# Gathers, node work and the last sums of a graph layer: where the copy of x runs and how the last two chunks are cut

## The chip, the cores and the metric

The kernel runs on one core of a Trainium2 chip. The metric is the device time of one execution in microseconds (us). Before the change the median of three runs is 1359.61 us (1357.78 to 1359.88). A core has five engines with queues of their own: TensorE (PE: matrix products and transposes), VectorE (DVE), ScalarE (ACT), GpSimd (POOL) and SyncE (SP, which here only issues DMAs).

## The reference

A layer on a graph of N = 8192 nodes with C = 256 channels and E = 131072 edges sorted by target, in float32 throughout:

```python
ea = edge_attr @ w_e + b_e
msg = jax.nn.relu(x[src] + ea)
agg = jax.ops.segment_sum(msg, dst, num_segments=N)
t = x + agg
h_local = _bn(jax.nn.relu(t @ w1 + b1) @ w2 + b2 + x, bn1_g, bn1_b)
# attention inside groups of 32 nodes, 4 heads
h_attn = _bn(attention(x) @ out_w.T + out_b + x, bn2_g, bn2_b)
out = h_local + h_attn
out = _bn(out + (jax.nn.relu(out @ m_w1 + m_b1) @ m_w2 + m_b2), bn3_g, bn3_b)
return _layernorm(x + out)
```

So each edge fetches the row of its source node, adds its own 64 features times `w_e` and a bias, takes a relu, and is summed into its target. Attention needs x alone; the dense layers need the sums.

## The kernel before, in words

**Edges** go in NB = 128 blocks of 1024. Since targets are sorted, block b touches about 64 nodes, and its sums fall into a window of 160 nodes that begins 48 before node 64 b. For each block, `gather` (L112) has POOL issue 8 indirect DMAs (L117) of 128 rows of 1 KB each into a buffer `xs` (5 buffers). `load_edges` (L127) loads the features of two blocks at once (`ea`, 2 buffers). `edge_transpose` (L410) turns them on PE and ACT copies them out. `edge_products` (L419) multiplies by `w_e` on PE (L428), DVE adds the gathered rows (L430) and ACT takes the relu (L433), each in two halves. `edge_sums` (L436) sums on PE with one-hot matrices that DVE makes (L440, L449), and ACT copies the result (`ws`, L454). `edge_place` (L457) moves the sums into the node window by another one-hot product (L463, L468), and DVE adds them to the transposed x of the chunk (L478), for two blocks together except for the last two blocks.

**The bias b_e** is added in one of two ways. `copy_x` (L482) makes a copy `xb` of x with b_e added: a chunk of 512 nodes is loaded (L491), DVE adds `be` (L492), and it is stored to HBM (L486). Gathers of blocks from NX = 13 on read `xb`. The first 13 blocks read x itself, and DVE adds `be` to each half of their messages (L432, two instructions a block). `copy_x(i)` handles two chunks, so all 16 chunks are called for within blocks 0 to 8. Its tiles share the buffers of tiles of the dense layers (tags h1, zT, and y with two buffers).

**Nodes** go in 16 chunks of 512. `attention` (L237) and `dense` (L335) are generators: they yield after each piece with a price in us. `Work` (L494) keeps two streams of them, attention in one and dense in the other, and `run(us)` hands out pieces by turns until the amount is used up. A piece that yields `LATER` (after the softmax on DVE) lets its stream rest for three calls of `run`. `dense` can do a part of a chunk: tiles `t_a` to `t_z` of its four tiles of 128 nodes. Its layers are at L344, ACT's relus at L351 and L360, DVE's adds at L354 and L369, its transposes at L381, the layer norm at L384 to L392, its store at L395.

**Order.** On PE the instructions run in the order in which the program is written (`manual_schedule`, L537). On the other engines and in the DMA queues a scheduler orders them at build time, and each then runs strictly in that order. The main loop (L546) handles block b so: load the features of b + 2, copy x, gather b + 2, products of b, a third of `PER` (4.875 us) of node work, sums of b - 1, a third, transpose of b + 2, a third, and place all sums up to b - 2 (up to b - 1 from block 126 on). The dense layers of chunk c - 1 enter at block 8 c + 4, so those of chunk 14 at block 124; chunk 15 enters in parts at the ends of blocks 126, 127 and 128.

At the start `srcd` (L58) holds the source indices of the first two blocks, which the first 16 gathers read. Those of all other blocks come out of the setup as `srci`.

Of the kernel before, what the change touches and what calls it, by code (L numbers as in the profile page):

```python
# [9 lines left out]
FP = mybir.dt.float32  # L10
# [8 lines left out]
P = 128  # L19
N, C, E, ED, H, NPG = 8192, 256, 131072, 64, 4, 32  # L20
DH = C // H
KC = C // P
BE = 1024
NB = E // BE
NH = 4
WN = P // NH
TJ = BE // NH // P
TB = NH * TJ
NPB = N // NB
WB = 160  # L30
WL = 48
CH = 512
NCH = N // CH
BPC = NB // NCH
TN = CH // P
GT = P // NPG
NX = 13
ND = 2
AGG_ROWS = N + 2 * P
TE = 8  # L40
# [9 lines left out]
def gnn_kernel(ctx: ExitStack, tc: tile.TileContext, x, src, dst, edge_attr, w, out):  # L50
    nc = tc.nc
# [3 lines left out]


    srcd = const.tile([P, ND * NH, TJ], I32, name="srcd")
    nc.sync.dma_start(srcd, src[0 : ND * BE].rearrange("(g p j) -> p g j", p=P, j=TJ))  # L58


    ident = const.tile([P, P], FP, name="ident")
# [8 lines left out]
    xb = dram.tile([N, C], FP, name="xb")  # L70
# [8 lines left out]
    w1 = const.tile([P, KC, C], FP, name="w1")  # L79
    w2 = const.tile([P, KC, C], FP, name="w2")  # L80
    mw1 = const.tile([P, KC, 2 * C], FP, name="mw1")
    mw2 = const.tile([P, 2 * KC, C], FP, name="mw2")
# [24 lines left out]
    npool = fast.enter_context(tc.tile_pool(name="node", bufs=1))  # L107
# [4 lines left out]
    def gather(b):  # L112
        xs = epool.tile([P, NH, TJ, C], FP, name="xs", tag="xs", bufs=5)
        for h in range(NH):
            for j in range(TJ):
# [3 lines left out]
                    out_offset=None,  # L119
                    in_=x if b < NX else xb[:, :],  # L120
                    in_offset=bass.IndirectOffsetOnAxis(ap=idx, axis=0),
# [213 lines left out]
    def dense(n0, st, pool, bank, t_a=0, t_z=TN):  # L335

        nt = t_z - t_a
        cs, ts, part = slice(t_a * P, t_z * P), slice(t_a, t_z), nt / TN
        xn, tT, hA = st["xn"][:, ts, :], st["xT"][:, :, cs], st["hA"][:, :, cs]

        def layer(wt, nk, o, act):
            ps = bank()[:, : nt * P]
            for k in range(nk):
                nc.tensor.matmul(  # L344
                    ps, wt[:, k, o * P : (o + 1) * P], act[:, k, :], start=(k == 0), stop=(k == nk - 1)
                )
            return ps

        h1 = pool.tile([P, KC, CH], FP, name="h1", tag="h1")[:, :, : nt * P]
        for o in range(KC):  # L350
            nc.scalar.activation(h1[:, o, :], layer(w1, KC, o, tT), AF.Relu, bias=v_("b1", o))  # L351
            yield 1.7 * part
        for o in range(KC):
            nc.vector.scalar_tensor_tensor(  # L354
                hA[:, o, :], layer(w2, KC, o, h1), s1[:, o : o + 1], hA[:, o, :], op0=ALU.mult, op1=ALU.add
            )
            yield 1.7 * part
        m1 = pool.tile([P, 2 * KC, CH], FP, name="m1", tag="m1")[:, :, : nt * P]
        for o in range(2 * KC):
            nc.scalar.activation(m1[:, o, :], layer(mw1, KC, o, hA), AF.Relu, bias=v_("m_b1", o))  # L360
            yield 1.7 * part
        zT = pool.tile([P, KC, CH], FP, name="zT", tag="zT")[:, :, : nt * P]
        for o in range(KC):

            nc.scalar.activation(
                zT[:, o, :], hA[:, o, :], AF.Identity, scale=s3[:, o : o + 1], bias=c3[:, o : o + 1]
            )
        for o in range(KC):
            nc.vector.scalar_tensor_tensor(  # L369
                zT[:, o, :], layer(mw2, 2 * KC, o, m1), s3[:, o : o + 1], zT[:, o, :], op0=ALU.mult, op1=ALU.add  # L370
            )
            yield 3.4 * part
        y = pool.tile([P, TN, C], FP, name="y", tag="y", bufs=2)[:, :nt, :]
        st6 = pool.tile([P, TN, 6], FP, name="st", tag="st")
        mv = pool.tile([P, TN, 2], FP, name="mv", tag="mv")
        for t2 in range(0, nt, 2):
            n2 = min(2, nt - t2)
            ps = bank()[:, : n2 * C].rearrange("p (t c) -> p t c", t=n2)
            for t in range(n2):
                for k in range(KC):  # L380
                    nc.tensor.transpose(  # L381
                        ps[:, t, k * P : (k + 1) * P], zT[:, k, (t2 + t) * P : (t2 + t + 1) * P], ident
                    )
            nc.vector.tensor_add(y[:, t2 : t2 + n2, :], ps, xn[:, t2 : t2 + n2, :])  # L384
        for t in range(nt):
            nc.vector.bn_stats(st6[:, t, :], y[:, t, :])
            nc.vector.bn_aggr(mv[:, t, :], st6[:, t, :])
        rstd = pool.tile([P, TN], FP, name="rstd", tag="rstd")
        nc.scalar.activation(rstd[:, :nt], mv[:, :nt, 1], AF.Sqrt, bias=eps_t)
        nc.vector.reciprocal(rstd[:, :nt], rstd[:, :nt])  # L390
        for t in range(nt):
            nc.vector.tensor_scalar(  # L392
                y[:, t, :], y[:, t, :], mv[:, t, 0:1], rstd[:, t : t + 1], ALU.subtract, ALU.mult
            )
        nc.sync.dma_start(out[ds(n0 + t_a * P, nt * P), :].rearrange("(t p) c -> p t c", p=P), y)  # L395
        yield 0.9 * part
# [3 lines left out]
    chunk = [{} for _ in range(NCH)]  # L400

    def bank():
        return pps.tile([P, CH], FP, name="at", tag="at", bufs=2)
# [75 lines left out]

    xp_of = {}  # L480

    def copy_x(i):  # L482

        for c in range(2 * i - 2, 2 * i):
            if c >= 0:
                nc.sync.dma_start(xb[c * CH : (c + 1) * CH, :].rearrange("(p t) c -> p t c", p=P), xp_of.pop(c))  # L486
        for c in range(2 * i, min(2 * i + 2, NCH)):

            tag = ("h1", "y", "zT", "y")[c % 4]
            xp = xp_of[c] = npool.tile([P, TN, C], FP, name="xp", tag=tag, bufs=2 if tag == "y" else 1)  # L490
            nc.sync.dma_start(xp, x[c * CH : (c + 1) * CH, :].rearrange("(p t) c -> p t c", p=P))  # L491
            nc.vector.tensor_add(xp, xp, be[:, None, :].to_broadcast([P, TN, C]))  # L492

    class Work:  # L494
# [20 lines left out]
        def run(self, us):  # L515
            self.owed += us
            for i in range(2):
                self.rest[i] = max(self.rest[i] - 1, 0)
            while self.owed > 0:
                ready = [i for i in (self.turn, 1 - self.turn) if self.streams[i] and not self.rest[i]]  # L520
                if not ready:
                    break
                t = self.piece(ready[0])
                if t == LATER:
                    self.rest[ready[0]] = 3
                elif t is not None:
                    self.owed -= t
                    self.turn = 1 - ready[0]
            self.owed = min(self.owed, 2.0)
# [5 lines left out]
    work = Work()  # L535
    PER = 39.0 / BPC
    with tc.manual_schedule(engines={PE}):  # L537
        first = [attention(c * CH, chunk[c], npool, bank, bank2) for c in range(2)]
        for g in first:
            next(g)  # L540
        for g in first:
            work.add(0, g)
        edge_transpose(0)
        edge_transpose(1)
        placed = 0
        for b in range(NB + 1):  # L546
            if b + 2 < NB:
                load_edges(b + 2)
            if b <= NCH // 2:
                copy_x(b)  # L550
            if 4 <= b < 8:
                wt, name = ((w1, "w1"), (w2, "w2"), (mw1, "m_w1"), (mw2, "m_w2"))[b - 4]
                nc.sync.dma_start(wt, w[name].rearrange("(k p) m -> p k m", p=P))
            if b + 2 < NB:
                gather(b + 2)
            c, at = divmod(b, BPC)
            if at == 0 and 1 <= c < NCH - 1:
                work.add(0, attention((c + 1) * CH, chunk[c + 1], npool, bank, bank2))
            if at == 4 and 1 <= c < NCH:
                work.add(1, dense((c - 1) * CH, chunk[c - 1], npool, bank))  # L560
            if b < NB:
                edge_products(b)
            work.run(PER / 3)
            if b >= 1:
                edge_sums(b - 1)
            if b < NB:
                work.run(PER / 3)
            if b + 2 < NB:
                edge_transpose(b + 2)
            if b < NB:  # L570
                work.run(PER / 3)

            while placed <= (b - 2 if b < NB - 2 else b - 1):
                edge_place(placed)
                placed += 1
            if b == NB - 2:
                work.add(1, dense((NCH - 1) * CH, chunk[NCH - 1], npool, bank, 0, 2))
            if b == NB - 1:
                work.add(1, dense((NCH - 1) * CH, chunk[NCH - 1], npool, bank, 2, 3))
        work.add(1, dense((NCH - 1) * CH, chunk[NCH - 1], npool, bank, 3, 4))  # L580
        work.finish()
    fast.close()

# [120 lines left out]
```

## Time and profile before

The profile is of one execution that took 1364.3 us, of which the recorded span is 1362.5 us; the median of the plain runs is 1359.61 us.

| engine | busy us | share of the span | instructions |
|---|---|---|---|
| PE | 1242.5 | 91% | 7939 |
| POOL | 995.5 | 73% | 1032 |
| DVE | 743.0 | 55% | 1218 |
| ACT | 662.5 | 49% | 1014 |

The page cuts the span into 40 slices of 34 us. In the first three the DMA engines are busy for 8 or 9 tenths and more (283, 361 and 352 GB/s moved), afterwards for 4 or 5 tenths. PE is busy 9 tenths or more from the ninth slice on to the fourth from the end. POOL is at 7 tenths in nearly all slices and falls to 4 and 0 in the last two. The mean clock granted to PE is 0.977.

How to read it: "L117" is line 117 of the kernel. Groups of instructions give the count, the busy time, the mean of one in ns, and the idle time ahead of them with what ended it. "Issue" as a reason means that the engine waited for nothing that the profile shows. In the timelines each row gives start, duration, engine, line, operation, and in brackets the idle time before it.

### The profile page before, as it was taken

How to read it: one execution, taken by the hardware profiler on the slowest of the kernel's cores; microseconds unless marked ns; L12 is line 12 of the kernel's file. 1: busy time of each engine (PE TensorE's matmuls, PEld its weight loads, DVE VectorE, ACT ScalarE, POOL GpSimd, SP SyncE). 2: the span in 40 equal slices, each digit the busy share in tenths (PEclk: the TensorE clock that was granted, in tenths of full speed). 3: DMA queues.
4: the chain of work that ended last, by engine and by line, in shares of the span. 5: the costliest groups of instructions: out<-in, count | busy, mean ns of one | idle time of the engine just before them, and what ended most of it. 6: DMA issues, size and time to landing. Idle time of an engine off the chain costs nothing.

```text
span 1362.5 us, 20476 instructions
## 1 busy us (share of the span) xinstructions
PE 1242.5 (91%) x7939; PEld 738.2 (54%) x7939; DVE 743.0 (55%) x1218; ACT 662.5 (49%) x1014; POOL 995.5 (73%) x1032
## 2 busy tenths in 40 slices
PE   2778979899999999999999999999999999999797
PEld 2445545555556555555555555555556565565455
DVE  5687665545556463645546464555645555545452
ACT  1444444545555564545546465454645455554332
POOL 6877777777777777777777777777777777777740
PEclk9889989899999999999999999999999999999899
DMA  8994445445454454545454454544545454454421
GB/s 283 361 352 116 130 117 160 141 136 153 135 169 137 126 161 136 167 136 152 136 148 138 137 165 137 151 136 140 162 123 167 135 164 123 137 148 123 137 62 33
DMA packets 141443, 206.73 MB, mean 152 GB/s; under 512 B 19710, under 2 KB 103964, under 8 KB 141340
## 3 DMA queue, kind: packets, MB, share of 16 engines
q0 software_dynamic: 49152, 134.28, 34.6%
q1 hardware_dynamic: 90768, 69.75, 16.0%
q10 hardware_dynamic: 1420, 1.33, 0.3%
q8 instruction: 64, 1.05, 0.3%
q14 instruction: 39, 0.32, 0.1%
HBM read 188.51 MB, written 16.78 MB: 151 GB/s over the span
## 4 chain that ended last, share of the span: by engine, by line
PE 43%; POOL 23%; issue 12%; DVE 8%; DMA 8%; ACT 5%; SPq 0%; DVEq 0%; POOLq 0%; ACTq 0%
POOL xs L117 23%; PE at L344 15%; PE pe L428 8%; DMA xs<-xb,srci 6%; PE pw L449 4%; PE at L256 4%; DVE msg L430 3%; PE l L468 3%; PE at L266 2%; PE at L327 2%; PE tp L414 2%; ACT msg L433 2%; PE at L315 1%; DVE bd L307 1%; ACT pr L292 1%
## 5 line engine op out<-in xcount | busy, mean ns | idle before, releaser
L117 POOL DMA_INDIRECT xs<-xb,srci x920 | 879.3, 956 | 280.3 <-issue 264.5
L433 ACT ACTIVATE msg<-msg 128x1024 f32<-128x1024 f32 x256 | 269.4, 1056 | 361.1 <-DVE msg L430 309.7
L430 DVE TENSOR_TENSOR msg<-pe,xs 128x1024 f32<-128x1024 f32 x256 | 303.5, 1219 | 62.6 <-PE pe L428 44.0
L428 PE MATMUL pe<-we,eaT 64*128 64x256 f32 x2048 | 263.8, 397 | 1.1 <-ACT pr L292 0.8
L428 PEld LDWEIGHTS pe<-we,eaT 64*128 64x128 f32 x2048 | 190.6, 191 | 46.7 <-issue 20.2
L449 PE MATMUL pw<-msg,oh 128*32 128x256 f32 x2048 | 139.1, 390 | 0.0
L344 PE MATMUL at<-hA,mw 128*128 128x512 f32 (+2 forms) x288 | 127.8, 567 | 5.8 <-DVE hA L354 5.4
L256 PE MATMUL at<-xT,inT 128*128 128x512 f32 x256 | 126.0, 615 | 5.9 <-DVE y L384 4.0
L344 PE MATMUL at<-m,mw 128*128 128x512 f32 (+2 forms) x288 | 117.9, 554 | 6.6 <-ACT xT L246 6.5
L117 POOL DMA_INDIRECT xs<-in_x_dram,srci x88 | 98.7, 1121 | 26.8 <-issue 26.2
L416 ACT COPY eaT<-tp 128x512 f32<-128x512 f32 x128 | 74.5, 582 | 86.7 <-PE tp L414 86.1
L414 PE MATMUL tp<-ident,ea 128*128 128x128 f32 x512 | 81.4, 282 | 35.4 <-ACT ws L454 32.4
L414 PEld LDWEIGHTS tp<-ident,ea 128*128 128x128 f32 x512 | 60.6, 143 | 92.4 <-ACT ws L454 56.6
L449 PEld LDWEIGHTS pw<-msg,oh 128*32 128x32 f32 x2048 | 54.0, 110 | 100.6 <-issue 45.0
L468 PEld LDWEIGHTS l<-oh,ws 128*128 128x128 f32 x512 | 82.3, 195 | 39.5 <-issue 36.9
L440 DVE TENSOR_TENSOR oh<-iota_n,rel 128x256 f32<-128x256 f32 x128 | 54.1, 423 | 75.7 <-PE pw L449 75.6
L468 PE MATMUL l<-oh,ws 128*128 128x160 f32 x512 | 94.2, 308 | 0.5 <-ACT ws L454 0.5
L369 DVE SCALAR_TENSOR_TENSOR zT<-at,s,zT 128x512 f32<-128x512 f32 (+2 forms) x36 | 24.9, 692 | 123.4 <-PE at L344 122.1
L463 DVE TENSOR_SCALAR oh<-iota_n,wrow 128x160 f32<-128x160 f32 x128 | 41.6, 325 | 84.9 <-PE l L468 84.8
L344 PEld LDWEIGHTS at<-m,mw 128*128 128x128 f32 x288 | 49.9, 190 | 57.9 <-issue 45.8
L478 DVE TENSOR_TENSOR xT<-l,xT 128x352 f32<-128x352 f32 (+3 forms) x95 | 42.2, 464 | 62.6 <-PE l L468 62.4
L344 PEld LDWEIGHTS at<-hA,mw 128*128 128x128 f32 x288 | 47.5, 190 | 50.4 <-issue 34.1
(106 smaller groups left out, 1313.8 us busy)
## 6 DMA issues: line engine op xcount, KB each, us to landing
ea<-in_edge_attr_dram SPq DMA_DIRECT2D x64, 512.0 KB, 4.5
xs<-xb,srci POOLq DMA_INDIRECT x920
xn<-in_x_dram SPq DMA_DIRECT2D x16, 512.0 KB, 5.0
xp<-in_x_dram SPq DMA_DIRECT2D x16, 512.0 KB, 6.5
xb<-xp SPq DMA_DIRECT2D x16, 512.0 KB
out_dram<-y SPq DMA_DIRECT2D x15, 512.0 KB, 3.2
xs<-in_x_dram,srci POOLq DMA_INDIRECT x88
mw<-in_L_gnn_m_w_dram SPq DMA_DIRECT2D x2, 512.0 KB
```

Of the source, the lines that this page charges most:

```text
L117: nc.gpsimd.indirect_dma_start(out=xs[:, h, j, :], out_offset=None, in_=x if b < NX else xb[:, :], in_offset=bass.IndirectOffsetOnAxis(ap= ...
L256: nc.tensor.matmul(ps, inT[:, k, o * P : (o + 1) * P], xT[:, k, :], start=(k == 0), stop=(k == KC - 1))
L344: nc.tensor.matmul(ps, wt[:, k, o * P : (o + 1) * P], act[:, k, :], start=(k == 0), stop=(k == nk - 1))
L414: nc.tensor.transpose(tp[:, h, :], ea[:, h, :], ident)
L416: nc.scalar.copy(eaT, tp)
L428: nc.tensor.matmul(pe[:, i, u, :], eaT[rows, h + u, :], we[rows, :], start=True, stop=True)
L430: nc.vector.tensor_add(half, pe, xs[:, h : h + 2].rearrange("p u i c -> p i u c"))
L433: nc.scalar.activation(msg[:, h : h + 2], msg[:, h : h + 2], AF.Relu)
L440: nc.vector.tensor_tensor(oh, iota_n[:, None, :WN].to_broadcast([P, TB, WN]), rel[:, b, :, None].to_broadcast([P, TB, WN]), ALU.is_equal,)
L449: nc.tensor.matmul(pw[h * WN : (h + 1) * WN, :], oh[:, h * TJ + j, :], msg[:, h, j, :], start=(j == 0), stop=(j == TJ - 1),)
L468: nc.tensor.matmul(l2[:, k, odd * NPB : odd * NPB + WB], ws[:, k * P : (k + 1) * P], oh2, start=(not odd and k == 0), stop=bool(odd or alo ...
L478: nc.vector.tensor_add(xT, l2[:, :, a - n : z - n], xT)
```

## The change

Six edits go together.

1. `NX` is 22 instead of 13: nine more blocks gather from x and have their bias added on DVE (L432).
2. `srcd` is loaded by two DMAs, the half of block 0 from SP and that of block 1 from ACT.
3. `copy_x` handles one chunk a block over blocks 0 to 16, with the tags h1 and zT alone, one buffer each. The loads of the four dense weights move from blocks 4 to 7 to blocks 7 to 10.
4. Within a block the transposes of b + 2 stand behind both pieces of node work (a third and two thirds of the amount, in two calls), and a resting stream rests for two calls. In the last 8 blocks the amount is 1.3 times as large.
5. The sums of b - 1, not b - 2, are placed from block 116 on.
6. Chunk 14's dense layers run in two halves that enter as soon as their sums are placed (ends of blocks 118 and 122), chunk 15's as before in parts.

```diff
-NX = 13
+NX = 22
...
-    nc.sync.dma_start(srcd, src[0 : ND * BE].rearrange("(g p j) -> p g j", p=P, j=TJ))
+    for b in range(ND):
+        (nc.sync, nc.scalar)[b].dma_start(
+            srcd[:, b * NH : (b + 1) * NH, :], src[b * BE : (b + 1) * BE].rearrange("(g p j) -> p g j", p=P, j=TJ)
+        )
...
-    def copy_x(i):
-
-        for c in range(2 * i - 2, 2 * i):
-            if c >= 0:
-                nc.sync.dma_start(xb[c * CH : (c + 1) * CH, :].rearrange("(p t) c -> p t c", p=P), xp_of.pop(c))
-        for c in range(2 * i, min(2 * i + 2, NCH)):
-
-            tag = ("h1", "y", "zT", "y")[c % 4]
-            xp = xp_of[c] = npool.tile([P, TN, C], FP, name="xp", tag=tag, bufs=2 if tag == "y" else 1)
+    def copy_x(c):
+
+        if c >= 1:
+            nc.sync.dma_start(xb[(c - 1) * CH : c * CH, :].rearrange("(p t) c -> p t c", p=P), xp_of.pop(c - 1))
+        if c < NCH:
+
+            xp = xp_of[c] = npool.tile([P, TN, C], FP, name="xp", tag=("h1", "zT")[c % 2])
             nc.sync.dma_start(xp, x[c * CH : (c + 1) * CH, :].rearrange("(p t) c -> p t c", p=P))
             nc.vector.tensor_add(xp, xp, be[:, None, :].to_broadcast([P, TN, C]))
...
                 if t == LATER:
-                    self.rest[ready[0]] = 3
+                    self.rest[ready[0]] = 2
...
-            if b <= NCH // 2:
+            if b <= NCH:
                 copy_x(b)
-            if 4 <= b < 8:
-                wt, name = ((w1, "w1"), (w2, "w2"), (mw1, "m_w1"), (mw2, "m_w2"))[b - 4]
+            if 7 <= b < 11:
+                wt, name = ((w1, "w1"), (w2, "w2"), (mw1, "m_w1"), (mw2, "m_w2"))[b - 7]
...
+            per = PER if b < NB - 8 else 1.3 * PER
             if at == 0 and 1 <= c < NCH - 1:
                 work.add(0, attention((c + 1) * CH, chunk[c + 1], npool, bank, bank2))
-            if at == 4 and 1 <= c < NCH:
+            if at == 4 and 1 <= c < NCH - 1:
                 work.add(1, dense((c - 1) * CH, chunk[c - 1], npool, bank))
             if b < NB:
                 edge_products(b)
-            work.run(PER / 3)
+            work.run(per / 3)
             if b >= 1:
                 edge_sums(b - 1)
             if b < NB:
-                work.run(PER / 3)
+                work.run(2 * per / 3)
             if b + 2 < NB:
                 edge_transpose(b + 2)
-            if b < NB:
-                work.run(PER / 3)
-
-            while placed <= (b - 2 if b < NB - 2 else b - 1):
+
+            while placed <= (b - 2 if b < NB - 12 else b - 1):
                 edge_place(placed)
                 placed += 1
-            if b == NB - 2:
-                work.add(1, dense((NCH - 1) * CH, chunk[NCH - 1], npool, bank, 0, 2))
-            if b == NB - 1:
-                work.add(1, dense((NCH - 1) * CH, chunk[NCH - 1], npool, bank, 2, 3))
-        work.add(1, dense((NCH - 1) * CH, chunk[NCH - 1], npool, bank, 3, 4))
+
+            for c, t_a, t_z in ((NCH - 2, 0, 2), (NCH - 2, 2, 4), (NCH - 1, 0, 2), (NCH - 1, 2, 3), (NCH - 1, 3, 4)):
+                need = -(-(c * CH + t_z * P + WL) // NPB)
+                need += need % 2 if need < NB - 2 else 0
+                if b == min(need, NB):
+                    work.add(1, dense(c * CH, chunk[c], npool, bank, t_a, t_z))
         work.finish()
```

The number of gathers (1024), of products and of chunks is the same in both. Line numbers in what follows are those of the kernel before.

## The prediction

> **What bounds the kernel now.** I read the page's engine rows first, then POOL's waits, then timelines of POOL, DVE and PE at the start, around block 12 and at the end. By busy share PE looks like the bound. It isn't the one that sets the end:
>
> ```profile
> PE 1242.5 (91%) x7939; PEld 738.2 (54%) x7939; DVE 743.0 (55%) x1218; ACT 662.5 (49%) x1014; POOL 995.5 (73%) x1032
> ...
> L117 POOL DMA_INDIRECT xs<-xb,srci x920 | 879.3, 956 | 280.3 <-issue 264.5
> ```
>
> ```profile
> POOL xs L117 <- issue: 295.2, 969, 0.3
> ...
> POOL xs L117 <- DMA srcd<-in_src_dram: 4.6, 1, 4.6
> ```
>
> Columns of the second: who waited for what, us in all, times, longest. After a first wait of 4.6 us, no idle time of POOL is longer than 0.3 us, and that gap stands before each gather. POOL waits for no buffer and no copy: it issues 1024 gathers end to end, at 6.16 to 1312.35 us. A plain one takes 0.946 + 0.30 = 1.25 us; 1024 make 1280.0, and 6.16 + 1280.0 leaves 26.2 us by which some gathers are longer. So span = 6.16 + 1280 + 26.2 + 50.2, the last being what follows the last gather's end, which I call X = 1312.35. Each term is judged below; PE may catch up or fall back in between without effect, as long as POOL never waits for it.
>
> **The lengthened gathers.** The excess is 14.3 us before 100 us, 5.7 from 100 to 200, then about 0.7 per 100. They fall together with two DVE instructions:
>
> ```profile
> 57.27 0.94 POOL L117 DMA_INDIRECT xs<-in_x_dram,srci  x1 [0.30 <-issue]
> 58.51 0.95 POOL L117 DMA_INDIRECT xs<-in_x_dram,srci  x1 [0.30 <-issue]
> 59.76 1.98 POOL L117 DMA_INDIRECT xs<-in_x_dram,srci  x1 [0.30 <-issue]
> ```
>
> ```profile
> 58.45 1.22 DVE L430 TENSOR_TENSOR msg<-pe,xs 128x1024 f32<-128x1024 f32 x1
> 59.71 1.22 DVE L432 TENSOR_TENSOR msg<-msg,be 128x1024 f32<-128x1024 f32 x1
> ```
>
> The gather that starts 0.05 us into an L432 takes 1.98 us, 1.03 too much; the one beside L430 (one input in PSUM) takes 0.95. This recurs: a gather that starts under L432, L492 or another addition with both inputs in SBUF ends about 0.8 us after it. [...]
>
> Edit 1 adds 18 L432, in blocks 13 to 21 (about 198 to 280 us). In blocks 5 to 12, past most of the copy, the excess of gathers under L432 and under the L440 right behind it adds up to 4.9 us, or 0.61 a block; blocks 13 to 21 have 0.01 from these now. Nine blocks: **+5.5 us**. Bounds: 0.28 (block 12) and 0.84 (block 11) a block, so 2.5 to 7.6. PE and DVE have room for the 22 us of added DVE time. The 16 L492 stay as they are, each costing POOL 0.5 in the mean.
>
> **srcd.** The 1024 pieces of 8 bytes move from 1.75 to 5.5 us. In the first 0.5 us, alone, 291 go; then the broadcast of b_e from ACT's queue enters and they drop to some 200 per us. Now half is awaited, and b_e stands behind the other half. [...] By the row of the first 0.5 us, all 1024 pass in 1.8 us instead of 3.75. I take the row: **-2.0 us** (0 to -2.4), straight off POOL's start.
>
> **The copy and the queues.** In the built order SP isn't spread as the loop reads: 14 of the 16 copies stand before the features of blocks 10 and 11, in DVE's order up to block 5, so they still crowd the first 110 us; only chunks 14 and 15 come at DVE's blocks 13 and 16. Fewer bytes in flight gain POOL nothing, since its excess is DVE's. Two costs hide behind margins. First, the buffers: gather b + 5 needs block b's `xs`, free when the second L430 ends. The tightest place:
>
> ```profile
> 190.74 1.22 DVE L430 TENSOR_TENSOR msg<-pe,xs 128x1024 f32<-128x1024 f32 x1
> ```
>
> ```profile
> 195.93 0.95 POOL L117 DMA_INDIRECT xs<-xb,srci  x1 [0.30 <-issue]
> ```
>
> Block 12 frees at 191.96, block 17's first gather starts at 195.93: 4.0 us, and 5.2 to 6.3 in the next three blocks. POOL's earlier start takes 2.0 of it, and in blocks 13 to 15 an L432 between the two L430 takes 1.2 more. Second, the copy itself: gather 22 needs chunk 15 stored. Its load waits for chunk 0's transposes, behind two feature loads in SP's queue (due by then):
>
> ```profile
> 228.86 1.14 PE L381 MATMUL at<-ident,zT 128*128 128x128 f32 x8
> ```
>
> So 230.0, plus 5.0 for a load of that size (`xn`), 1.2 for L492, 3.2 to 6.5 to land: 240 to 243. Block 22's first gather is at 246.1 now, less 2.0, plus some 3 from L432. A margin of 4 to 7 us; cost 0. DVE, which waits in order for these two loads, delays blocks 14 and 17 by 1 to 2 us, inside the same margins.
>
> **Transposes behind both pieces, shares of `run`.** These take PE's stalls for the shared PSUM buffer (PE and its weight loads on "tp" for ACT's `ws`: up to 57 us in all). PE runs some 30 us behind POOL at first (block 0's products begin at 40.8) and has caught up by block 80 or so. Caught up earlier it waits for gathers: 0. Earlier placing (edit 5) and chunk 14's halves fill PE's idle time in blocks 121 to 125; worth only what they leave undone at the end.
>
> **The end.** In the order of now, after block 127's products PE still has chunk 14's last layer, sums 126 and transposes (1317.07 to 1323.14, 6.1 us), then chunk 15's first half, its third tile from 1338.55, its fourth from 1347.41:
>
> ```profile
> 1315.14 2.00 PE L428 MATMUL pe<-we,eaT 64*128 64x256 f32 x16
> 1317.07 3.70 PE L344 MATMUL at<-m,mw 128*128 128x512 f32 x8
> ...
> 1338.55 0.61 PE L344 MATMUL at<-xT,w 128*128 128x128 f32 x4
> ...
> 1355.51 0.33 PE L381 MATMUL at<-ident,zT 128*128 128x128 f32 x1 [0.40 <-DVE zT L369]
> ```
>
> In the new order chunk 14 is done, and the first half of chunk 15 stands right behind block 127's products, which can go about 6 us before X (they need only block 126's additions). It looks as if that half (some 13 us) would vanish in the wait for the last gather. It doesn't: in ACT's built order the second relu of the first layer (L351) stands behind the second relu half of block 127 (L433), which needs the last gather. Block 124 shows that now:
>
> ```profile
> 1277.79 3.70 PE L344 MATMUL at<-xT,w 128*128 128x512 f32 x8
> 1287.18 3.78 PE L344 MATMUL at<-h,w 128*128 128x512 f32 x4 [5.69 <-ACT h L351]
> ```
>
> Its last gather ended at 1282.3, and the second layer could start 4.9 us later. So from X: +4.8 to the second layer; 1.5 for what remains of it and 0.6 for DVE's addition; third layer 4.1 and sums 126, 1.1; fourth 3.6 and placing 126, 0.7; addition and transposes 1.2; sums 127, wait and placing, 2.3: 19.9. Then as now 9.0 (1338.55 to 1347.57) and 8.3 for the two tiles, and 6.7 from the last transpose (1355.84) to the end. 43.9 in place of 50.2: **-6.3 us** (-4.5 to -7.5).
>
> **Sum.** +5.5 - 2.0 - 6.3 = -2.8: a span of 1359.7. The profiled execution took 1364.3 with its surroundings, 4.7 over the median; taking the difference over to the median: **1356.8 us**. About 0.2% (2.7 us) is what a measurement can tell from no change, so this is just beyond it. The bounds of the terms make about -7 to +2.
>
> **Rivals.**
> - *The start falls back and POOL waits for a buffer* (slower). Copies use two buffers, so two chunks a round: load (6.5 us to landing in the crowded start), addition 1.2, store some 4.5 and gaps, 12.7 us; chunk 12 in the seventh round, at about 115 us, while DVE holds block 5's second addition behind it (now at 106). At 11 us a round, which lighter traffic would allow, it costs 1 or 2 us. Every us of lag beyond 2 (4.0 less 2.0) is POOL's for good; from 5 on the change loses. With 8 us of lag: -2.8 + 6 = +3.2, 1362.8. For it: DVE waited 15.7 us for such loads even with four buffers. Against: DVE has five fewer L492 up to block 3, and starts block 1 some 4 us earlier.
> - *L432 costs POOL nothing there* ([...] gathers fall into gaps): -8.3, 1351.3. Against it stands block after block up to 12.
> - *The first half of chunk 15 does hide*: 7.9 us less at the end, -10.7, 1348.9. Against it is ACT's order.
> - *The copy isn't spread*, as worked out: costs nothing either way, and is within the forecast.
>
> **Chances.** Forecast 0.56, POOL waiting 0.22, L432 free 0.13, half hidden 0.09. Within the forecast 0.35 is faster by over 0.2%, 0.16 within, 0.05 slower; of the second 0.03 within and 0.19 slower; the others faster but for 0.01. So 0.56 faster, 0.20 same, 0.24 slower. Range 1350 to 1364: it holds the forecast's own (1352.5 to 1361.5), most of the slower case, and the free L432.
>
> **What would show it.** First gather at about 4.2 us; in blocks 13 to 21 (until 280 us) gathers 5.5 us longer in sum; POOL's longest later wait still 0.3 us; last gather ending near 1315.9; 44 us from there to the end, with PE idle before the second layer of chunk 15 for ACT's L351. A POOL wait for DVE's L430 between blocks 17 and 21, or for `xb` at block 22, would make it wrong, as would an end 36 or 50 us behind the last gather.

## The result and the profile after

The changed kernel takes **1379.01 us** (median of four, 1376.08 to 1380.46), the kernel before beside it 1359.55: a ratio of 1.0143, with an interval of 1.0122 to 1.0164. That is 19 us slower where 2.8 us faster was forecast, and outside the range of 1350 to 1364. Line numbers are those of the changed kernel unless said otherwise: up to `copy_x`, three more than before (L430 is L433, L315 is L318). Eleven of the runs told below fell on chips on which the kernel before itself took some 1910 us at a granted clock of 0.87; they are set against it alone and have a section of their own.

First the page, its rows on the engines, the chain of waits and the gathers:

```profile
PE 1248.6 (91%) x7987; PEld 749.9 (54%) x7987; DVE 768.1 (56%) x1241; ACT 662.8 (48%) x1023; POOL 1001.6 (73%) x1032
...
PE 51%; POOL 14%; DVE 12%; DMA 8%; issue 8%; ACT 6%; DVEq 0%; ACTq 0%; POOLq 0%
...
L120 POOL DMA_INDIRECT xs<-xb,srci x848 | 811.5, 957 | 258.3 <-issue 246.7
```

The shares of busy time say nothing: TensorE is at 91% as before. Neither do those of the chain: TensorE's part is 51% where it was 43% and POOL's 14% where it was 23%, but the fastest kernel below (the changed one with the old copy and a rest of three) has 52% and 14%. What tells is the times. POOL's waits (what for, us in all, times, longest):

```profile
POOL xs L120 <- issue: 296.1, 972, 0.3
POOL xs L120 <- DVE msg L433: 18.3, 19, 4.6
...
POOL xs L120 <- DMA srcd<-in_src_dram: 1.6, 1, 1.6
```

The last line is edit 2: 1.6 us in place of 4.6. The middle one is new in its length: before, none was over 0.3. In POOL's timeline (start, duration, engine, line, operation, idle time before it) the three longest are:

```profile
107.23 2.02 POOL L120 DMA_INDIRECT xs<-in_x_dram,srci  x1 [4.06 <-DVE msg L433]
...
165.93 1.81 POOL L120 DMA_INDIRECT xs<-in_x_dram,srci  x1 [3.66 <-DVE msg L433]
...
203.19 1.81 POOL L120 DMA_INDIRECT xs<-in_x_dram,srci  x1 [4.58 <-DVE msg L433]
```

Each is the first gather of a block, and it waits for a buffer that VectorE has not yet given back. With smaller ones they make 12.4 us beyond the usual gap. With that and 6.1 us more of lengthened gathers, less 3.0 of the earlier start, the last gather ends at 1327.9 us instead of 1312.3.

VectorE itself stands longer for the loads of the copy, 32.8 us in all where it was 15.7. Before and after:

```profile
DVE xp L492 <- DMA xp<-in_x_dram: 15.7, 10, 4.2
```

```profile
DVE xp L493 <- DMA xp<-in_x_dram: 32.8, 10, 6.7
```

I read every trace of this study by the same four terms as the prediction did, all from POOL's timeline: where the first gather starts, by how much gathers are longer than 0.946 us in sum, what POOL waits beyond its gaps, and what follows the last gather. The last two columns tell how far the second message addition of a block ends behind the block's last gather, at blocks 12 and 112. All values are us.

| profiled kernel | first gather | longer gathers | POOL waits | last gather ends | from there to the end | span | behind at 12 | behind at 112 |
|---|---|---|---|---|---|---|---|---|
| before | 6.2 | 25.8 | 0.0 | 1312.3 | 50.2 | 1362.5 | 39.2 | 9.5 |
| changed | 3.2 | 31.9 | 12.4 | 1327.9 | 50.8 | 1378.7 | 51.9 | 20.4 |
| changed, rest of 3 | 3.2 | 35.1 | 0.0 | 1318.8 | 43.4 | 1362.2 | 26.5 | 5.1 |
| changed, old copy | 3.2 | 21.6 | 2.4 | 1307.5 | 54.3 | 1361.8 | 44.6 | 25.6 |
| changed, old copy, rest of 3 | 3.2 | 24.4 | 0.0 | 1308.2 | 43.7 | 1351.9 | 29.2 | 4.3 |
| before, new order alone | 5.8 | 26.9 | 0.0 | 1313.0 | 47.0 | 1360.0 | 37.5 | 20.4 |
| before, new copy alone | 6.0 | 30.9 | 0.3 | 1317.5 | 50.4 | 1367.9 | 43.3 | 9.0 |
| before, NX = 22 alone | 5.8 | 30.5 | 0.0 | 1316.7 | 49.2 | 1365.9 | 40.1 | 9.3 |
| before, new end and srcd | 3.3 | 25.0 | 4.4 | 1313.1 | 42.7 | 1355.8 | 48.0 | 13.2 |

Each row is one execution. That of the kernel before took 4.7 us more than its median, and that of the changed kernel with the old copy 3.9 us less than its own (1363.57, the fastest of six); the others lie within 1.5 us of theirs. Differences between those two rows and others are uncertain by as much.

The second row says where to look: not only did POOL lose 12.4 us, the end behind the last gather is no shorter either, and TensorE, which had all but caught up before, is 20 us behind at block 112. The same shows in its pace. From block 28 to 80 the products of a block (L431) follow each other every 9.70 us before and 10.05 after, and POOL's gathers of a block every 10.06 in both. So before, TensorE gained on POOL; now it merely keeps up. The windows of these 52 blocks, before and after (stretch, its length, busy time of PE, its weight loads, DVE, ACT and POOL with counts, granted clock, DMA share and GB/s):

```profile
341.87:846.32 504.45, 491.72 (x3162) 285.81 (x3161) 275.97 (x452) 266.46 (x402) 382.28 (x402) 1.00 0.50 145
```

```profile
354.10:876.76 522.66, 497.19 (x3161) 287.93 (x3161) 278.33 (x452) 266.83 (x402) 396.23 (x416) 0.98 0.50 143
```

Of the 18.2 us more, 12.7 are idle time of TensorE; in the other 5.5 the same products take longer, at a granted clock of 0.98 instead of 1.00.

**What it waits for.** In the list of TensorE's waits between 200 and 800 us the score products (`bd`, the transposed softmax that VectorE makes) stand out, before and after:

```profile
PE tp L414 <- ACT ws L454: 7.5, 9, 3.6
...
PE at L315 <- DVE bd L307: 1.6, 2, 1.4
```

```profile
PE at L318 <- DVE bd L310: 16.7, 5, 4.9
...
PE tp L417 <- ACT ws L457: 4.8, 4, 3.1
```

Edit 4 took 2.7 us of the waits for `tp` in this stretch and put 15.1 us of waits for `bd` in their place. TensorE's timeline of block 28 shows how, first before, then in the changed kernel:

```profile
341.87 2.00 PE L428 MATMUL pe<-we,eaT 64*128 64x256 f32 x16
...
347.43 1.07 PE L449 MATMUL pw<-msg,oh 128*32 128x256 f32 x16
348.43 1.98 PE L344 MATMUL at<-h,w 128*128 128x512 f32 x4
350.25 0.60 PE L414 MATMUL tp<-ident,ea 128*128 128x128 f32 x4
351.01 1.09 PE L315 MATMUL at<-bd,vn 128*64 128x128 f32 x16 [0.16 <-DVE bd L307]
```

```profile
354.10 2.00 PE L431 MATMUL pe<-we,eaT 64*128 64x256 f32 x16
356.03 3.70 PE L347 MATMUL at<-xT,w 128*128 128x512 f32 x8
359.66 1.07 PE L452 MATMUL pw<-msg,oh 128*32 128x256 f32 x16
363.36 1.09 PE L318 MATMUL at<-bd,vn 128*64 128x128 f32 x16 [2.63 <-DVE bd L310]
364.38 3.45 PE L347 MATMUL at<-h,w 128*128 128x512 f32 x4
367.76 1.27 PE L318 MATMUL at<-bd,vn 128*64 128x128 f32 x16
...
370.10 2.00 PE L431 MATMUL pe<-we,eaT 64*128 64x256 f32 x16
```

VectorE ends the transposes behind `bd` (2.85 us, L310) at 363.2, 9.1 us after the block's products begin, just as before: both message additions of the block stand among the steps of the softmax. What has moved is TensorE's asking. Before, the stream was let loose in the third call of `run`, behind the transposes (L414), and asked 9.0 us after the products began. Now the last two calls are one, ahead of the transposes; the stream is let loose in it, right behind the sums (L452), and asks after 6.6 us. A rest of two calls is one block now as a rest of three was before, but it ends one place earlier. Block 28 to 29 takes 16.0 us, 12.7 before.

### The profile page after: what moved, and what is told of

Its sections match the earlier page's. It is cut to its first block, busy times and chain, and to the rows that moved or that the text cites. A ratio compares the mean times of both kernels' runs of the same rounds, so it can differ in the third digit from the quotient of the medians.

```text
span 1378.7 us, 20604 instructions
## 1 busy us (share of the span) xinstructions
PE 1248.6 (91%) x7987; PEld 749.9 (54%) x7987; DVE 768.1 (56%) x1241; ACT 662.8 (48%) x1023; POOL 1001.6 (73%) x1032
## 4 chain that ended last, share of the span: by engine, by line
PE 51%; POOL 14%; DVE 12%; DMA 8%; issue 8%; ACT 6%; DVEq 0%; ACTq 0%; POOLq 0%
PE at L347 17%; POOL xs L120 14%; PE pe L431 10%; PE pw L452 5%; DVE msg L433 4%; PE at L259 4%; PE at L330 3%; DMA xp<-in_x_dram 3%; PE l L471 3%; PE at L269 3%; PE tp L417 3%; ACT msg L436 2%; DVE bd L310 2%; PE at L318 2%; DMA xs<-xb,srci 2%
## 5 line engine op out<-in xcount | busy, mean ns | idle before, releaser
L120 POOL DMA_INDIRECT xs<-xb,srci x848 | 811.5, 957 | 258.3 <-issue 246.7
L433 DVE TENSOR_TENSOR msg<-pe,xs 128x1024 f32<-128x1024 f32 x256 | 303.8, 1217 | 49.8 <-PE pe L431 34.2
L431 PE MATMUL pe<-we,eaT 64*128 64x256 f32 x2048 | 262.7, 395 | 1.5 <-ACT pr L295 1.4
L120 POOL DMA_INDIRECT xs<-in_x_dram,srci x160 | 173.0, 1081 | 61.2 <-issue 45.1
L431 PEld LDWEIGHTS pe<-we,eaT 64*128 64x128 f32 x2048 | 189.9, 190 | 45.1 <-issue 15.8
L452 PE MATMUL pw<-msg,oh 128*32 128x256 f32 x2048 | 138.8, 389 | 0.0
L452 PEld LDWEIGHTS pw<-msg,oh 128*32 128x32 f32 x2048 | 53.8, 110 | 98.7 <-issue 39.2
L347 PEld LDWEIGHTS at<-m,mw 128*128 128x128 f32 x304 | 53.4, 190 | 61.6 <-issue 48.2
L347 PEld LDWEIGHTS at<-hA,mw 128*128 128x128 f32 x304 | 51.8, 190 | 61.6 <-issue 45.6
L259 PEld LDWEIGHTS at<-xT,inT 128*128 128x128 f32 x256 | 44.9, 191 | 63.3 <-issue 46.4
```

Of the source, the lines that this page charges most:

```text
L120: nc.gpsimd.indirect_dma_start(out=xs[:, h, j, :], out_offset=None, in_=x if b < NX else xb[:, :], in_offset=bass.IndirectOffsetOnAxis(ap= ...
L259: nc.tensor.matmul(ps, inT[:, k, o * P : (o + 1) * P], xT[:, k, :], start=(k == 0), stop=(k == KC - 1))
L347: nc.tensor.matmul(ps, wt[:, k, o * P : (o + 1) * P], act[:, k, :], start=(k == 0), stop=(k == nk - 1))
L431: nc.tensor.matmul(pe[:, i, u, :], eaT[rows, h + u, :], we[rows, :], start=True, stop=True)
L433: nc.vector.tensor_add(half, pe, xs[:, h : h + 2].rearrange("p u i c -> p i u c"))
L452: nc.tensor.matmul(pw[h * WN : (h + 1) * WN, :], oh[:, h * TJ + j, :], msg[:, h, j, :], start=(j == 0), stop=(j == TJ - 1),)
```

## The experiments

Two theories were written down. **START**: the loss is that of the start, the slower copy rounds, the longer gathers and POOL's waits. **PACE**: a rest of two calls makes TensorE ask for `bd` too early, it falls behind, and it sets the end. Where the expectations put the waits for `bd` at 66 us after and 33 before, they add TensorE's row and that of its weight loads, which count largely the same waits twice; on TensorE alone they are 37.2 and 15.2 over the whole run.

### The changed kernel with the old copy

```diff
-NX = 22
+NX = 13
...
-    def copy_x(c):
+    def copy_x(i):
...
-            if 7 <= b < 11:
+            if 4 <= b < 8:
```

> The changed kernel with edits 1 and 3 taken back (old copy through four buffers, NX = 13), beside a kernel before that takes 1360 us. START: POOL's waits for DVE's L433 vanish (12.5 us beyond the usual gaps), as do 6 us of lengthened gathers; last gather ends near 1310, time about 1354. PACE: PE begins 11 us earlier but still needs 10.05 us a block and stays 20 us and more behind POOL to the end: about 1368.

Measured: 1367.43 us (1363.57 to 1370.42), beside it 1360.83 before: a ratio of 1.0065 (1.0044 to 1.0087). PACE holds. With the start set right POOL's last gather ends 4.8 us earlier than in the kernel before, and yet the time is 0.65% above it. The trace shows one reason: 54.3 us follow that gather, the longest end of all. It doesn't show all of it, since it is of the fastest of the six executions and its span is no longer than that of the trace before.

### A rest of three calls

```diff
                 if t == LATER:
-                    self.rest[ready[0]] = 2
+                    self.rest[ready[0]] = 3
```

> The changed kernel with the rest of a block's step raised from 2 calls to 3; nothing else differs. PACE: TensorE's waits for bd are nearly gone, blocks 28 to 80 take 9.7 us each again instead of 10.05, TensorE is back within 10 us of the gathers at the last block, and what is left is the slow start: 1368 to 1372 us. START: the time stays at 1379.

> The changed kernel with the old copy of x (two chunks a round, 13 blocks, weights in the old places) and the rest of a block's step at 3 calls; the load of the indices in two halves, the transposes behind both pieces and the new end stay. PACE: the last gather ends near 1307.5 us, as with the old copy alone, TensorE's waits for bd are nearly gone, it is back within 8 us of the gathers at the last block, and the end follows 44 to 50 us after them: 1352 to 1358 us. START or a dear new end: no gain over the old copy alone, 1367.

Measured: the changed kernel with this line alone 1363.71 us (1359.20 to 1366.04) beside 1363.12, a ratio of 1.0000 (0.9989 to 1.0011); with the old copy as well **1354.73 us** (1353.69 to 1357.28), 0.9945 (0.9926 to 0.9964), faster than both kernels of this case. One digit is worth the whole loss: 1.4% with the new copy, 1.2% with the old one (1.0065 to 0.9945). It doesn't put the rest back to what it was: three calls were one block before and are one and a half now, so it also takes away waits for `bd` that the kernel before had. The first run's expectation was missed, 1368 to 1372, because the gain is larger than PACE said; and blocks 28 to 80 take 10.01 us each there, not 9.7, since TensorE has caught up with POOL by block 40 (4.8 us behind) and follows its pace.

In the first, both misses of the changed kernel go away together. POOL's list has no buffer wait over the usual gap left, and the end is 43.4 us:

```profile
POOL xs L120 <- issue: 295.9, 971, 0.3
...
POOL xs L120 <- DVE msg L433: 1.5, 5, 0.3
```

TensorE's timeline of block 28 and 29 in the second:

```profile
322.55 2.28 PE L431 MATMUL pe<-we,eaT 64*128 64x256 f32 x16
...
328.39 1.07 PE L452 MATMUL pw<-msg,oh 128*32 128x256 f32 x16
329.92 3.70 PE L347 MATMUL at<-h,w 128*128 128x512 f32 x8 [0.45 <-ACT h L354]
...
334.53 2.00 PE L431 MATMUL pe<-we,eaT 64*128 64x256 f32 x16
336.46 1.09 PE L318 MATMUL at<-bd,vn 128*64 128x128 f32 x16
```

The score products now come in the next block, behind its products, and wait for nothing. Over the whole run TensorE's waits for `bd` shrink to 1.8 us in both. The gain is largest where PACE did not place it, at the start: block 12's products begin at 170.2 us with the new copy, 198.1 in the changed kernel and 187.2 before. At block 12 a part of this is work put off (40 of TensorE's products come later), but by block 28 the number done is the same and the lead on the changed kernel is still 28.3 us: from block 0's products on, 21.5 us less idle time, and 7.8 us less for the same products at a granted clock of 0.97 instead of 0.92. That is worth more than the prediction's margin of 4 us, and more than the new copy's rounds cost: these are as late here or later (chunk 13's addition at 120.4 us, 114.9 in the changed kernel; VectorE waits 28.6 us for the loads), and POOL still waits for no buffer.

### The new order alone

```diff
-                    self.rest[ready[0]] = 3
+                    self.rest[ready[0]] = 2
...
-                work.run(PER / 3)
+                work.run(2 * PER / 3)
...
-            if b < NB:
-                work.run(PER / 3)
```

> The kernel before with the new order of a block's step alone (transposes behind both pieces of node work, two calls a block, a rest of 2). PACE: the rest of two alone makes TensorE ask for the score products too early, its waits for bd are 50 us or more against 33, it comes 10 to 25 us behind the gathers at the last block as with the old copy (16 us), and the end follows: with the old end's 50 us, 1366 to 1373 us. If it hurts only together with the other edits: 1358 to 1363.

Measured: 1361.13 us (1357.50 to 1364.21) beside 1359.58, a ratio of 1.0011 (1.0002 to 1.0020). **PACE in its plain form falls.** Its first half is there: TensorE waits 32.5 us for `bd` and is 20.4 us behind at block 112. But at block 124 it is 3.1 us behind, and the end does not suffer. With the old copy and the new end it is 25.6 behind at block 112 and still 24.1 at block 124. What differs is in the windows from block 112's products to block 124's, of this kernel and then of the changed one with the old copy (columns as above):

```profile
1178.50:1280.50 102.00, 97.80 (x669) 58.60 (x668) 61.37 (x106) 53.96 (x81) 77.35 (x81) 1.00 0.51 146
```

```profile
1178.90:1298.00 119.10, 115.58 (x751) 72.72 (x750) 67.83 (x123) 60.99 (x96) 90.17 (x96) 1.00 0.48 143
```

POOL needs 120 us for twelve blocks. With the old end TensorE has 97.8 us of work in them, and makes up 17 us of its lag. The new end (chunk 14's halves, and 1.3 times the work of a block) puts 17.8 us more in the same place, and nothing can be made up. The lag is nearly harmless with the old end (0.1%), and the new end is cheap without a lag, as the next run shows; together they cost.

### The new end and srcd alone

```diff
+            per = PER if b < NB - 8 else 1.3 * PER
...
-            while placed <= (b - 2 if b < NB - 2 else b - 1):
+            while placed <= (b - 2 if b < NB - 12 else b - 1):
...
+            for c, t_a, t_z in ((NCH - 2, 0, 2), (NCH - 2, 2, 4), (NCH - 1, 0, 2), (NCH - 1, 2, 3), (NCH - 1, 3, 4)):
```

> The kernel before with the load of the indices in two halves and the new end (last two chunks' dense layers in parts, last sums placed at once, 1.3 times the work of a block in the last eight), under the old order and the old copy. If the new end is only dear when TensorE comes to it late: TensorE is 5 to 10 us behind the gathers at block 112 as in the kernel before, the last gather ends near 1309 us and the end follows 43 to 47 us later: 1352 to 1358 us. If the new end is dear by itself: 1362 to 1367, as with the old copy alone.

Measured: 1357.48 us (1352.35 to 1358.60) beside 1360.30, a ratio of 0.9972 (0.9962 to 0.9982). The new end is not dear by itself: it is 42.7 us long. The end of the gathers was missed: 1313.1, not 1309. POOL started 3 us earlier, TensorE was 48 us behind at block 12, and POOL gave 4.4 us back in one wait for a buffer at block 17. An early start is worth something only if TensorE comes along, which it does with a rest of three (last gather at 1308.2).

### The new copy, and NX, alone

The first run has edits 1 and 3, the second this line of edit 1 alone:

```diff
-NX = 13
+NX = 22
```

> The kernel before with the new copy of x alone (one chunk a round over 16 blocks, two slots, weights from block 7, 22 blocks that gather from the input), under the old order of a step. PACE: the gathers grow by 9 us in all as in the run with a rest of three, POOL waits for no buffer, its last gather ends near 1321.6 us: 1367 to 1371 us. START: POOL waits for buffers as well, 12 us: 1378 to 1384.

> The kernel before with 22 blocks that gather from the input instead of 13, so with 18 more additions of the bias on VectorE beside the gathers; the copy of x stays as it was. If the additions alone make the gathers longer: 7 to 9 us more in all, 1366 to 1369 us. If part of it is the new copy rounds' (their additions fall on other gathers, up to block 16): 4 to 6 us more, 1364 to 1366.

Measured: the whole of edits 1 and 3 alone 1369.65 us (1368.04 to 1371.27) beside 1359.58, 1.0072 (1.0043 to 1.0100); NX alone 1367.93 us (1367.47 to 1368.57) beside 1360.30, 1.0056 (1.0037 to 1.0075). The two intervals overlap, and both traces have the same excess of gathers, 30.9 and 30.5 us. So the price is that of the 18 additions of the bias; taken alone, the copy in rounds of one chunk adds nothing that these runs can tell, though VectorE waits 26.9 us for its loads. It gives nothing back either: the new copy is a pure loss here. Over the traces of the table, five with 13 such blocks have 24.7 us of longer gathers in the mean (21.6 to 26.9), four with 22 have 32.1 (30.5 to 35.1): 7.4 us.

### The same kernels where the kernel before takes 1910 us

In these runs TensorE's own work took longer (1402 us busy in a profile of the new order alone, 1242.5 before) and POOL waited throughout: in that profile it stands 744 us idle ahead of the 920 gathers from the copy (280 before), 449 of them for VectorE's additions, and the granted clock is 0.868. Some us lost at the start or the end of the gathers can't be read there.

> The changed kernel with one number put back: a resting attention stream rests for three calls of run, not two (one and a half blocks, since a block now has two calls). Theory PACE (the softmax gets too little time before attention's next products, so PE stands still once a chunk, runs a block in 10.05 us instead of 9.70, and never catches POOL up): PE's waits for bd before L318 fall from 66 us to at most 33, PE has caught up with POOL by about block 115, the end is 44 us behind the last gather (1328) instead of 51, time about 1372. Theory START (only the delays of the first 20 blocks count, since POOL's queue sets the end): 1379 as it is, within 2 us.

> The changed kernel with edits 1 and 3 taken back (copy of two chunks a block through four buffers, weights at blocks 4 to 7, NX = 13); srcd, order, rest and tail as changed. START: POOL's waits for DVE's L433 vanish (12.5 us beyond the usual gaps), as do 6 us of lengthened gathers; last gather ends near 1310, and with the new tail the time is about 1354. PACE: PE begins 11 us earlier but still needs 10.05 us a block, so it stays 20 us and more behind POOL to the end: about 1368.

> The kernel before with edits 1 and 3 alone (one chunk a block through two buffers, weights at blocks 7 to 10, NX = 22). START: POOL waits for L430 in blocks 8 to 17, some 9 to 12 us (it starts 3 us later than in the changed kernel, which leaves it that much more room), gathers 6 us longer; last gather near 1328, and 50 us after it: about 1376 to 1378. If edit 4 were the only cause: at most 1365 (6 us for the longer gathers).

> The kernel before with edit 4 alone (transposes behind both pieces, two calls of run a block, rest of two calls; no larger amount at the end). PACE: waits for bd grow to some 60 us, PE stays 25 to 30 us behind POOL through the middle and is late at the end: about 1370, though POOL's last gather still ends near 1312. START: as before, 1359.6 within 2 us.

> The kernel before with edits 2, 5 and 6 alone (srcd in two loads, earlier placing at the end, chunk 14 in halves, 1.3 times the amount in the last 8 blocks); copy, NX, order within a block and rest as before. If the terms of the prediction for these edits hold: POOL starts 3.0 us earlier, as in the changed kernel's trace, the last gather ends near 1309.5, and 44 us follow: 1353.5, so about 9 us less than before. If the tail is worth nothing: 1357.

> The changed kernel with the old copy of x (two chunks a round, 13 blocks, weights in the old places) and the rest of a block's step at 3 calls: the load of the indices in two halves, the transposes behind both pieces and the new end stay. PACE: both costs are gone; POOL starts 3 us earlier than before and its last gather ends near 1307.5 us, as in the run with the old copy alone; if TensorE is back within 8 us of it the end follows 44 to 50 us later: 1352 to 1358 us. START: the old copy alone had already taken away all that can be had: 1367, as measured with it.

| kernel | ratios to the kernel before on the same chip, with intervals |
|---|---|
| changed, rest of 3 | 0.984 (0.976 to 0.992), 0.978 (0.967 to 0.989), 0.984 (0.974 to 0.994) |
| changed, old copy | 0.984 (0.977 to 0.991), 0.973 (0.966 to 0.980) |
| new copy alone | 0.994 (0.990 to 0.999), 1.018 (1.006 to 1.030) |
| new order alone | 0.988 (0.981 to 0.995), 0.988 (0.983 to 0.992) |
| new end and srcd | 0.999 (0.995 to 1.003) |
| changed, old copy, rest of 3 | 1887.25 us beside 1912.20, without an interval |

The expectations were made for the other chips, and none can be judged by these times. Where a kernel has several ratios, the expectation is that of its first run; the later ones were made from the same theories. Two things can still be read. The new order gains 1.2% in both runs, and every kernel with it has a lower median than before; why was not tried. And with a rest of three no wait for `bd` is longer than 3.4 us on these chips too.

## Why the prediction was wrong, step by step

- **What bounds the kernel** (POOL's gathers, end to end): right for the kernel before, and for the changed one with a rest of three. It was treated as given, not as something that the change could end; in the changed kernel TensorE's lag makes POOL wait and sets what follows the last gather.
- **srcd, -2.0**: -2.6 to -3.0, beyond its bound of -2.4: the first gather starts at 3.2 or 3.3 us in every kernel with it, at 5.8 to 6.2 in those without. The row that the prediction took (291 pieces in the first 0.5 us) pointed the right way and was low by 0.6 to 1.0 us; these runs don't tell what of it comes from the second queue and what from waiting for half the pieces. Yet "straight off POOL's start" holds only where no buffer is late behind it: in the run with the new end and srcd alone it was given back at block 17.
- **The lengthened gathers, +5.5**: +7.4 in the mean of traces, within its bounds of 2.5 to 7.6. NX alone shows that it is the additions: nothing else differs there, and by the ratio it costs 7.6 us. If those additions cost POOL nothing, as the second rival has it, this run would have equalled the kernel before; it was 0.56% slower. The trace of the changed kernel shows it gather by gather: of the 46 longer than 1.15 us in its first 400 us, 22 end 0.80 to 0.83 us behind an addition of the bias to messages (L435); of the 54 that start under an addition of the gathered rows (L433), 52 take at most 0.95 us.
- **The margins of the buffers, cost 0**: 12.4 us. The rival named the wait, and had the rounds of the copy nearly right (12.7 us; measured 13.5, from chunk 0's addition at 27.25 to chunk 12's at 108.35) and what they do to VectorE (32.8 us of waits for the loads). But the copy alone made POOL wait 0.3 us, with a start 2.8 us later, and with a rest of three the whole change made it wait 0.0. The rest of two is needed for the loss, and neither the forecast nor the rival had it: TensorE asks for `bd` while VectorE, held by the copy, is late with it. The longest such wait, 8.1 us, ends at 90.98; at that place it is 3.7 before, 3.3 with the new order alone and 7.2 with the new copy alone. Block 12's products come 1.0 us earlier than before with the new order alone, 3.0 later with the new copy alone and 11.0 later in the changed kernel. How the 12.4 us divide among the earlier start, the copy and the rest was not tried.
- **"Caught up earlier it waits for gathers: 0"**: the step that failed. It counted the waits for `tp` that edit 4 takes away, and not what stands in their place: the two calls a block with a rest of two, which the prediction doesn't price at all, so no bound held it. In the changed kernel TensorE waits 37.2 us for `bd`, and from block 28 to 80 it gains 2 us on POOL, where it gained 20 before. The trace of before had the row: 15.2 us of waits for `bd`, 13.6 of them in three waits ahead of 200 us, the longest 7.9, and those are what a rest is for. Against a rest of three it costs 19 us by the ratios (1.0143 to 1.0000). Against the order of before it costs only 1.5 us when alone (1.0011): the zero was nearly right for edit 4 by itself, and wrong for the six edits together.
- **The end, -6.3**: -6.8 and -6.5 with a rest of three, and 7.5 shorter with the old order. The mechanism was right. From the timeline of the changed kernel with a rest of three:

```profile
1316.71 1.99 PE L347 MATMUL at<-xT,w 128*128 128x256 f32 x8
1318.76 0.70 PE L347 MATMUL at<-h,w 128*128 128x256 f32 x2
1323.45 2.93 PE L347 MATMUL at<-h,w 128*128 128x256 f32 x6 [3.99 <-ACT h L354]
```

The last gather ends at 1318.8, and the second layer goes on 4.65 us later behind ACT's relu; the prediction had 4.8. In the changed kernel itself the same place reads:

```profile
1336.71 2.00 PE L431 MATMUL pe<-we,eaT 64*128 64x256 f32 x16
1338.64 1.99 PE L347 MATMUL at<-xT,w 128*128 128x256 f32 x8
1340.68 0.70 PE L347 MATMUL at<-h,w 128*128 128x256 f32 x2
1341.99 1.56 PE L347 MATMUL at<-h,w 128*128 128x256 f32 x6 [0.61 <-ACT h L354]
```

Block 127's products begin 8.8 us behind the last gather (1327.9); with a rest of three they begin 4.0 us ahead of it (1314.79). Of the wait for ACT 0.61 us is left: TensorE now sets the time here, and the end is 50.8 us, no shorter than before. So this term came out only where TensorE had caught up, the same condition that the step above took for granted.

The account closes. From the changed kernel with a rest of three to that with two: 12.4 us of POOL's waits less 3.2 us of shorter gathers, and an end 7.4 us longer: 16.6, and the spans differ by 16.5 (1378.7 less 1362.2). And with a rest of three the forecast's own sum, with that trace's terms, is -3.0 + 9.3 - 6.8 = -0.5, where -2.8 was forecast and the spans differ by -0.3 (1362.2 and 1362.5), the trace of before being 4.7 us over its median; by the ratio (1.0000) the medians don't differ. A slip of the prediction's changes nothing of this: the bounds of its terms add up to -7.4 and +3.1, not to -7 and +2.

## What to carry over

When one engine sets the end, the slack of the next one is a stock that several edits draw from: here the step's order alone costs 0.1%, the earlier start and the fuller last blocks by themselves gain 0.3%, and the three together lose 0.65% (the changed kernel with the old copy). So price an edit of a planner's pauses by the waits that the pause prevents, and list for each "costs nothing" what else of the same change uses that cover. A rest counted in calls changes its meaning with the number of calls in a block and with what stands between them; the trace answers it, in the wait of the first instruction behind the rest.

## What the runs showed of the hardware

A long wait of TensorE can be paid twice. In the changed kernel, as before, it waits 7.92 us for `bd` in one place and then runs 32 score products in 3.68 us that take 1.97 at a granted clock of 1.00. Its timeline, and the windows around it (granted clock in the third value from the end):

```profile
189.37 3.68 PE L318 MATMUL at<-bd,vn 128*64 128x128 f32 x32 [7.92 <-DVE bd L310]
```

```profile
180.00:189.00 9.00, 1.45 (x22) 0.47 (x18) 8.94 (x12) 3.12 (x4) 6.87 (x8) 0.71 0.32 89
189.00:193.00 4.00, 3.63 (x33) 3.30 (x33) 0.74 (x2) 0.69 (x1) 3.09 (x4) 0.50 0.34 98
```

The clock is 0.50 from 189.0 to 193.0 us. From 50 us on TensorE has seven waits of over 4 us in the traces of the two kernels, three before (4.09, 5.69 and 7.92) and four after (4.13, 4.88, 7.92 and 8.08), and in the 3.5 us behind each the granted clock is 0.50, but for 0.58 behind that of 4.09. Below that the length of the wait alone doesn't decide it here: behind 3.71 us in the kernel before, 32 products took 1.97 at a clock of 1.00, and behind the 2.63 us of block 28 the clock was 0.56 from 364.3 to 367.8 us, where four products took 3.45 us that take 1.98 in the same block of the kernel before.

```profile
85.97 1.97 PE L315 MATMUL at<-bd,vn 128*64 128x128 f32 x32 [3.71 <-DVE bd L307]
```

From 100 to 200 us the mean granted clock is 0.88 in the changed kernel, 0.91 before and 1.00 with a rest of three and the old copy, and that is a part of the lead that the rest of three gives at the start.
